# A fourth inner product cut into seven in five of seven outer products, and the small sums on one engine

## The chip, the core and the metric

The kernel runs on one core of a Trainium2 chip. The metric is the device time of one execution in microseconds. A core has five engines that each work through their own program in order: TensorE (PE, matrix multiplications into PSUM), VectorE (DVE), ScalarE (ACT), GpSimd (POOL) and SyncE (SP, which here issues the DMAs). They wait for each other by semaphores.

## The reference, cut to what matters

Input x is 64 sequences of 64 tokens of 1024 numbers, 4096 tokens in all, float32 throughout. Two layers follow each other:

```
x = x + A[id] (B[id] x)                      # rank 16, one adapter per sequence
logits = Wr x + 5 * onehot(language)         # 8 experts
gates = softmax of the top two, else 0
x = x + W x + 2 * sum_e gate_e * Bm_e (A1_e x)   # W is 1024 x 1024
```

Nearly all of the arithmetic is W x (the kernel multiplies by W + I, which takes in the residual).

## The kernel before, in words

Tokens lie along the free dimension, features on the partitions. The 4096 tokens are eight blocks of 512, and two blocks at a time make a pass (`s` = 0 to 3, `NSUP` = 4). In a pass the product (W + I) x is done by a scheme of seven multiplications in the place of eight, nested three deep:

- Outer level: W is a 2 x 2 of quarters, and the operand is a 2 x 2 of two feature halves by two token blocks. Seven *outer products* `n`, in the order `ORDER = (1, 2, 6, 7, 5, 3, 4)`, multiply sums of quarters by sums of token blocks (`token_sum`). Their results go to SBUF accumulators `U` and `V` (tiles u, v) and to output tiles `o`.
- Inner level: each outer product is again done in seven *inner products* `k` (function `product`), each of 256 x 256 weights by 256 tokens: four multiplications of 128 x 128 weights by 256 columns. The inner sums of tokens are tiles `ti` (`inner_tokens`, on POOL after pass 0). The results gather in PSUM tiles `pa` and `pb`, and DVE adds them to the accumulators (function `leave`; ACT copies where there is nothing to add to).
- Third level, in passes 1 to 3 (`FINE` = 1): the inner product `k` = 2 is cut into seven again, the *finer product* (`fine_product`, PSUM tile `pf`): seven multiplications of 128 x 128 weights by 128 columns, in four parts (four, one, one, one) between which other products stand. After each of the first three parts ACT copies a finished block to SBUF (tile `cp`), because that block has to be added in a second place; at the end DVE adds `pf` to the accumulator (`leave`), and then three sums add the blocks of `cp` (`rest_`). Ahead of it three sums make the token differences `tt` (`begin_fine`), and the weight sums `sf` are needed (`fine_weights`): they are made on POOL in pass 1, kept in DRAM (`f_kept`), and loaded in passes 2 and 3.

In outer products 2, 3, 7 and 4 the gated low-rank term is added by more multiplications of 256 columns (`b_sb` with tiles hg, hd, he) into the same PSUM tile for `k` = 2, 3, 7 and 4.

Beside this, each pass prepares the next token blocks on TensorE: transposes of the gathered B rows (`pt`), a projection (`pb` with 32-wide strips), the adapter product (`px`, from the gathered A rows `ga`, four PSUM banks at once), the expert rows (`ph`) and the transposed gates (`pg`).

The inner weight sums (tiles `s`) are made in pass 0, kept in DRAM (`s_kept`) and streamed back in every later pass, through a ring of SBUF places. `slots` gives each tile name its number of buffers: among others 26 for the weights `s` (which `sf` shares), 2 each for `tt`, `cp`, `ga`; in PSUM 4 banks `l`, 2 `a` and 2 `b`.

The order of work is not written by hand. Each step is put in by `plan.add` with an estimated cost per engine, its reads and writes, its buffers and a due time `at`; `Plan.order` runs through them with those estimates and gives every engine one fixed order, and `Pinned` keeps it. Whatever the estimates say, an engine on the chip waits for the step that stands next.

Of the kernel before, what the change touches and what calls it, by code (L numbers as in the profile page):

```python
# [8 lines left out]
F32 = mybir.dt.float32  # L9
# [5 lines left out]
P = 128  # L15
# [166 lines left out]
def kernel(  # L182
# [71 lines left out]
    WHOLE = {(0, 1)}  # L254

    FINE = 1

    pe, dve = Pinned(tc, nc.tensor), Pinned(tc, nc.vector)
    act, pool, sp = Pinned(tc, nc.scalar), Pinned(tc, nc.gpsimd), Pinned(tc, nc.sync)
    engine = {"DVE": dve, "POOL": pool}  # L260

    slots = {
        "q": 7, "s": 26, "tt": 2, "cp": 2, "t5": 2, "t6": 2, "t7": 2, "t4": 2, "o": 3, "hg": 3, "hd": 3,
        "gb": 2, "ga": 2, "bt": 1, "bx": 1, "h": 1, "l": 4, "a": 2, "b": 2,
    }
    plan = Plan(slots, {"l"})
    const = ctx.enter_context(tc.tile_pool(name="const", bufs=1))
# [6 lines left out]
    def new(tag, shape, name):  # L274
        return pools[tag].tile(shape, F32, tag=tag, name=name)
# [387 lines left out]
    }  # L663
    m_q = {1: quarter[0, 0], 2: quarter[0, 1], 4: quarter[1, 1]}
    s_kept = tc.dram_tile([7, 7, P, QC * QO], F32, name="s_kept")
    f_kept = tc.dram_tile([7, P, QC * QO], F32, name="f_kept")

    def combine(out, a, b, op, at, engines):

# [33 lines left out]
    def weights(s, n, at):  # L703

        out = {}
        if s > 0:
            for i, m in enumerate(ORDER):
                out[m] = t = ("s", s, n, m)

                def fn(e, t=t, m=m):  # L710
                    made[t] = new("s", [P, QC, QO], f"s_{s}_{n}{m}")
                    sp.dma_start(made[t].rearrange("p c o -> p (c o)"), s_kept[n - 1, m - 1])

                plan.add({"SP": 0.1}, fn, [("kept", n, m)], [(t,)], at + i - 8, [("s", t)], kb=256)
            wt[n] = out
            if s >= FINE:
                fine_weights(s, n, out[2], at)
            return
        m = m_q[n]
        out = {1: m[0, 0], 2: m[0, 1], 4: m[1, 1]}  # L720
        for k, (u, v, op) in {
            5: ((1, 0), (1, 1), ALU.add),
            6: (5, (0, 0), ALU.subtract),
            7: ((0, 0), (1, 0), ALU.subtract),
            3: ((0, 1), 6, ALU.subtract),
        }.items():
            out[k] = ("s", s, n, k)
            uu = m[u] if isinstance(u, tuple) else out[u]
            vv = m[v] if isinstance(v, tuple) else out[v]
            combine(out[k], uu, vv, op, at - 4, POOL)  # L730
        for k in ORDER:
            t = out[k]

            def keep(e, t=t, k=k):
                sp.dma_start(s_kept[n - 1, k - 1], made[t].rearrange("p c o -> p (c o)"))

            plan.add({"SP": 0.1}, keep, [(t,)], [("kept", n, k)], at + 4, kb=256)
        wt[n] = out

    def fine_weights(s, n, a, at):  # L740

        t = ("sf", s, n)

        def blocks():
            made[t] = new("s", [P, QC, QO], f"sf_{s}_{n}")
            return made[t].rearrange("p c (o w) -> p (c o) w", w=P)

        def load(e):
            blocks()
            sp.dma_start(made[t].rearrange("p c o -> p (c o)"), f_kept[n - 1])  # L750

        def sums(e):
            f, w4 = blocks(), made[a].rearrange("p c (o w) -> p (c o) w", w=P)
            a11, a21, a12, a22 = (w4[:, x] for x in range(4))
            v = engine[e]
            v.tensor_tensor(f[:, 0], a21, a22, ALU.add)
            v.tensor_tensor(f[:, 1], f[:, 0], a11, ALU.subtract)
            v.tensor_tensor(f[:, 2], a11, a21, ALU.subtract)
            v.tensor_tensor(f[:, 3], a12, f[:, 1], ALU.subtract)

        def keep(e):
            sp.dma_start(f_kept[n - 1], made[t].rearrange("p c o -> p (c o)"))

        if s == FINE:
            plan.add({"POOL": 1.6}, sums, [(a,)], [(t,)], at - 3, [("s", t)], sb=True)
            plan.add({"SP": 0.1}, keep, [(t,)], [("fine", n)], at + 4, kb=256)
        else:
            plan.add({"SP": 0.1}, load, [("fine", n)], [(t,)], at - 6, [("s", t)], kb=256)
        wt[n]["fine"] = t


    def token_sum(s, n, at):
# [80 lines left out]
    def products(s):  # L853
# [10 lines left out]
        def at():  # L864
            return s * SLOTS + slot[0]
# [104 lines left out]

        fine = {}

        def begin_fine(n):

            t, (tx, tk) = ("tt", s, n), ti[n][2]

            def fn(e):
                made[t] = new("tt", [P, 4, P], f"tt_{s}_{n}")
                f, b = made[t], tx()
                b11, b21 = b[:, 0, :P], b[:, 1, :P]  # L980
                dve.tensor_tensor(
                    f[:, :2], b[:, :, P:], b[:, 0, :].rearrange("p (h t) -> p h t", t=P), ALU.subtract
                )
                dve.tensor_tensor(f[:, 2], f[:, 1], b11, ALU.add)
                dve.tensor_tensor(f[:, 3], b21, f[:, 2], ALU.subtract)

            plan.add({"DVE": 0.9}, fn, tk, [(t,)], at() - 3, [("tt", t)], sb=True)

        def fine_product(n, part_):


            ps, cp = ("pc", s, n), ("cp", s, n)
            a, f, t, (tx, tk) = wt[n][2], wt[n]["fine"], ("tt", s, n), ti[n][2]
            extra = hd[n][2] if n in (2, 3, 7, 4) and part_ == 3 else None
            oh = {2: 0, 3: 0, 7: 1, 4: 1}.get(n)

            def fn(e):
                if part_ == 0:
                    made[ps] = new("b", [P, QC, HT], f"pf_{s}_{n}")
                out = made[ps].rearrange("p o (h t) -> p (o h) t", t=P)  # L1000
                w4 = made[a].rearrange("p c (o w) -> p (c o) w", w=P)
                a11, a21, a12, a22 = (w4[:, x] for x in range(4))
# [14 lines left out]
                    )  # L1017
                if extra is not None:
                    for j in range(QC):
                        o = oh * 2 * QC + j  # L1020
                        pe.matmul(
                            made[ps][:, j], b1_sb[:, o * P : (o + 1) * P], extra[0](),
                            start=False, stop=True, skip_group_check=True,
                        )
# [1 line left out]
            reads = [(a,), (f,), (t,)] + tk + ([("b1",), extra[1]] if extra is not None else [])  # L1026
            plan.add(
                {"PE": (0.88, 0.22, 0.22, 0.22)[part_] + 0.86 * (extra is not None)}, fn, reads,
                [(ps,)], at(), [("b", ps)] * (part_ == 0),
            )  # L1030
            slot[0] += (0.5, 0.13, 0.13, 0.13)[part_]

            def copy(e):
                out = made[ps].rearrange("p o (h t) -> p (o h) t", t=P)
                if part_ == 0:

                    made[cp] = new("cp", [P, 4, P], f"cp_{s}_{n}")
                    act.copy(made[cp][:, 0::3], out[:, 1::2])
                else:
                    act.copy(made[cp][:, part_], out[:, 1])  # L1040

            if part_ < 3:
# [2 lines left out]
                    [(cp,)], at() - 4, [("cp", cp)] * (part_ == 0),  # L1045
                )
                return
            leave(n, ps, 0, ALL, (0,), True)
            region = qk(dest[n], 0, ALL, (0,))

            def rest_(e):
                o, c = q(dest[n], 0, ALL, (0,)), made[cp]
                c11, c21, c2 = o[:, 0, :P], o[:, 1, :P], o[:, 1]
                dve.tensor_tensor(c11, c11, c[:, 0], ALU.add)
                dve.tensor_tensor(c2, c2, c[:, 1:3].rearrange("p h t -> p (h t)"), ALU.add)
                dve.tensor_tensor(c21, c21, c[:, 3], ALU.add)

            plan.add({"DVE": 0.9}, rest_, [(cp,)] + region, region, at() - 4, sb=True)

        def done(n, i, cs, js):  # L1060

# [39 lines left out]
        def begin(n):  # L1101
# [10 lines left out]
                    gate_diff(s, at() - 2)  # L1112
                return
            inner_tokens(s, n, tokens[n], at())
            if s >= FINE:
                begin_fine(n)
            if n == 4:
                gate_diff(s, at() - 2)
            if n in (2, 7, 3, 4):
# [2 lines left out]
        def step(n, k):  # L1122
# [8 lines left out]
            if k in (1, 6, 5, 3):  # L1131
# [4 lines left out]
                    leave(n, ("pb2", s, n), 1, ALL, (1,), True)  # L1136
                if k == 5 and last(n):
                    leave(n, ps, 0, ALL, (1,))
            elif k == 2:
                product(n, ("pc", s, n), 2, True)  # L1140
                leave(n, ("pc", s, n), 0, ALL, (0,), True)
            else:
                product(n, ("pb2", s, n), k, k == 7)
                if k == 7 and last(n):
                    leave(n, ("pb2", s, n), 1, ALL, (1,))
                if k == 4:
                    leave(n, ("pb2", s, n), 1, ALL, (0,), True)
# [1 line left out]
                done(n, i, ALL, (j,))  # L1149


        whole_h = {}
        begin(ORDER[0])
        rest = []
        for n in ORDER:
            after = ORDER[ORDER.index(n) + 1] if n != ORDER[-1] else None
            if (s, n) in WHOLE:
# [5 lines left out]
                    if x == 1 and after is not None:  # L1163
                        begin(after)
                continue
            step(n, 1)
            if rest:
                step(*rest[0])
            if s >= FINE:
                fine_product(n, 0)  # L1170
            else:
                step(n, 2)
            if rest:
                step(*rest[1])
            if after is not None:
                begin(after)

            for x, k in enumerate((6, 7, 5)):
                if s >= FINE:
                    fine_product(n, 1 + x)  # L1180
                if s >= FINE and x == 2:
                    done(n, 0, ALL, (0,))
                step(n, k)
            rest = [(n, 4), (n, 3)] if last(n) else [(n, 3), (n, 4)]
        for k in rest:
            step(*k)

    for k, at in ((0, -60), (1, -42)):
        load(k, 0, at)
# [86 lines left out]
```

## Time and profile before

| | |
|---|---|
| median of 3 runs | 519.69 us (519.22 to 520.44) |
| the profiled execution | 518.82 us, of which the profile's span is 517.0 |
| TensorE busy | 502.6 us (97% of the span) |
| VectorE busy | 359.2 us (69%) |
| GpSimd busy | 183.8 us (36%) |
| ScalarE busy | 59.1 us (11%) |
| granted TensorE clock | full in all of the span |
| DMA | 104.73 MB, mean 203 GB/s |

All of the kernel's instructions are recorded under one line (L29), that of the helper `Pinned`, so the profile is read by tile names: `pa<-ti,s` is a multiplication into `pa` of token sums `ti` and weights `s`. A TensorE multiplication in float32 leaves two records, so an inner product of four is "x8". Start and duration are in us, those of single instructions in ns. The passes can be told apart by time: pass 0 until about 147 us, then 123 us each.

### The profile page before, as it was taken

Reading aid. Unit: us, or ns where it says so; the run is one execution under the profiler, and the core shown is the slowest. Engines: PE = TensorE matmul, PEld = TensorE weight load, DVE = VectorE, ACT = ScalarE, POOL = GpSimd, SP = SyncE. Lnnn points to the kernel's source line nnn. Section 1 sums busy time; section 2 is a strip of 40 time slices with the busy share of each in tenths; the row PEclk is TensorE's granted clock in tenths of the full one; section 3 lists DMA queues with packets and bytes.
Section 4 is the critical chain, followed back from the end, with each engine's and each line's share of the span. In section 5 each row is a group of like instructions: output and inputs, shape, how many; then the busy total and the mean of one; then the engine's idle time right before and its main releaser. Section 6 shows DMA issues by size and latency. Waiting matters only on the chain.

```text
span 517.0 us, 9064 instructions
## 1 busy us (share of the span) xinstructions
PE 502.6 (97%) x3558; PEld 441.3 (85%) x3558; DVE 359.2 (69%) x700; ACT 59.1 (11%) x144; POOL 183.8 (36%) x169
## 2 busy tenths in 40 slices
PE   2999999999999999999999999999999999999997
PEld 2857988889889988898888898899889899888886
DVE  0689998988853596656888558548679558654843
ACT  1111100002001111012101110101200111001100
POOL 4073058182534346333234303312423332524300
PEclk9999999999999999999999999999999999999999
DMA  7999275798576347926466724954655674660122
GB/s 260 372 367 402 89 264 215 269 327 289 178 236 221 102 124 273 364 96 213 175 204 223 226 103 128 370 175 116 210 184 153 180 219 114 212 183 22 57 107 81
DMA packets 57290, 104.73 MB, mean 203 GB/s; under 512 B 5280, under 2 KB 11424, under 8 KB 57248
## 3 DMA queue, kind: packets, MB, share of 16 engines
q1 hardware_dynamic: 54944, 95.77, 54.8%
q0 software_dynamic: 2304, 8.39, 4.7%
q8 instruction: 28, 0.46, 0.3%
q14 instruction: 14, 0.11, 0.1%
HBM read 72.68 MB, written 31.46 MB: 201 GB/s over the span
## 4 chain that ended last, share of the span: by engine, by line
PE 92%; DVE 3%; DMA 2%; issue 1%; POOL 1%; SPq 0%; POOLq 0%
PE pa L29 37%; PE pb L29 28%; PE ph L29 11%; PE pf L29 8%; PE px L29 3%; PE pw L29 3%; DMA x<-in_xT 2%; DVE o L29 1%; PE pt L29 1%; DVE t L29 1%; PE pg L29 1%; POOL ti L29 0%; DVE x L29 0%; DVE tt L29 0%; SPq L29 0%
## 5 line engine op out<-in xcount | busy, mean ns | idle before, releaser
L29 PE MATMUL pa<-ti,s 128*128 128x256 f32 x432 | 102.6, 381 | 0.0
L29 PE MATMUL pb<-ti,s 128*128 128x256 f32 x384 | 95.7, 380 | 0.1
L29 PEld LDWEIGHTS pa<-ti,s 128*128 128x128 f32 x432 | 79.4, 190 | 10.0 <-issue 0.2
L29 PEld LDWEIGHTS pb<-ti,s 128*128 128x128 f32 x384 | 70.5, 190 | 8.7 <-DVE o L29 0.3
L29 PE MATMUL ph<-a_sb,x 128*128 128x136 f32 x512 | 63.0, 279 | 0.2 <-issue 0.2
L29 PEld LDWEIGHTS ph<-a_sb,x 128*128 128x128 f32 x512 | 62.0, 190 | 1.1 <-issue 0.4
L29 POOL TENSOR_TENSOR ti<-x,ti 128x512 f32<-128x512 f32 x24 | 32.2, 1340 | 71.6 <-PE pb L29 70.7
L29 POOL TENSOR_TENSOR ti<-x 128x512 f32<-128x512 f32 x24 | 31.6, 1316 | 67.9 <-PE pb L29 44.0
L29 PE MATMUL pa<-x,s 128*128 128x256 f32 x216 | 52.0, 380 | 0.0
L29 DVE TENSOR_TENSOR x<-px,x 128x512 f32<-128x512 f32 x64 | 39.6, 682 | 11.7 <-PE px L29 8.3
L29 POOL TENSOR_TENSOR ti<-t,ti 128x512 f32<-128x512 f32 x18 | 25.6, 1421 | 55.9 <-PE pb L29 55.1
L29 PEld LDWEIGHTS pa<-x,s 128*128 128x128 f32 x216 | 39.8, 190 | 5.0 <-issue 0.2
L29 PE MATMUL pa<-t,s 128*128 128x256 f32 x168 | 41.1, 381 | 0.0
L29 ACT COPY cp<-pf 128x128 f32<-128x128 f32 (+1 forms) x63 | 19.0, 302 | 182.4 <-PE pf L29 161.8
L29 POOL TENSOR_TENSOR ti<-t 128x512 f32<-128x512 f32 x18 | 23.4, 1299 | 36.5 <-PE pb L29 29.3
L29 PEld LDWEIGHTS pa<-t,s 128*128 128x128 f32 x168 | 31.3, 190 | 4.3 <-issue 0.2
L29 DVE TENSOR_TENSOR o<-pb,o 128x512 f32<-128x512 f32 x35 | 24.1, 689 | 13.6 <-PE pb L29 12.8
L29 POOL TENSOR_TENSOR s<-w,w 128x512 f32<-128x512 f32 x12 | 17.1, 1428 | 35.5 <-DVE w L29 22.3
L29 DVE TENSOR_TENSOR o<-pa,u 128x512 f32<-128x512 f32 x32 | 21.9, 686 | 5.8 <-PE pa L29 4.3
L29 PE MATMUL pf<-tt,sf 128*128 128x128 f32 x126 | 24.6, 277 | 0.0
L29 PEld LDWEIGHTS pf<-tt,sf 128*128 128x128 f32 x126 | 21.7, 191 | 2.1
L29 DVE TENSOR_TENSOR x<-x,x 128x512 f32<-128x512 f32 x16 | 12.5, 798 | 12.6 <-PE ph L29 12.6
(141 smaller groups left out, 728.0 us busy)
## 6 DMA issues: line engine op xcount, KB each, us to landing
s<-s_kept SPq DMA_DIRECT2D x147, 256.0 KB, 3.3
x<-in_xT SPq DMA_DIRECT2D x15, 1024.0 KB, 7.7
out_T<-o SPq DMA_DIRECT2D x30, 512.0 KB, 3.1
s_kept<-s SPq DMA_DIRECT2D x28, 256.0 KB, 4.3
s_kept<-w SPq DMA_DIRECT2D x18, 256.0 KB, 5.4
w<-in_w SPq DMA_DIRECT2D x16, 256.0 KB, 8.0
sf<-f_kept SPq DMA_DIRECT2D x14, 256.0 KB, 2.7
f_kept<-sf SPq DMA_DIRECT2D x7, 256.0 KB, 3.6
```

Of the source, the lines that this page charges most:

```text
L29: return self._tc.keep_in_program_order(f(*args, **kwargs))
```

## The change: what it does

In outer products 1, 2, 6, 7 and 3 the inner product `k` = 4 is done as a finer product too, in passes 1 to 3 (list `FOURTH`; its PSUM tile comes from the banks `l`, its token side is the sum `ti` of `k` = 4). The last outer product of the last pass is excepted by a test, but 4 is not in the list.

The sums `tt` and the late additions of `cp` run on POOL for all finer products, where they ran on DVE. Weight sums `sf` are kept for two `k` per outer product. `s` gets a 27th place, `tt` and `cp` a third one, `ga` loses its second.

The interleaving changes as well: a list `going` holds the finer products that are under way, and `advance()` issues the next part of each after every inner product, so that the fourth's parts run on into the next outer product.

```diff
+    FOURTH = (1, 2, 6, 7, 3)
...
-        "q": 7, "s": 26, "tt": 2, "cp": 2, "t5": 2, "t6": 2, "t7": 2, "t4": 2, "o": 3, "hg": 3, "hd": 3,
-        "gb": 2, "ga": 2, "bt": 1, "bx": 1, "h": 1, "l": 4, "a": 2, "b": 2,
+        "q": 7, "s": 27, "tt": 3, "cp": 3, "t5": 2, "t6": 2, "t7": 2, "t4": 2, "o": 3, "hg": 3, "hd": 3,
+        "gb": 2, "ga": 1, "bt": 1, "bx": 1, "h": 1, "l": 4, "a": 2, "b": 2,
...
-    f_kept = tc.dram_tile([7, P, QC * QO], F32, name="f_kept")
+    f_kept = tc.dram_tile([7, 2, P, QC * QO], F32, name="f_kept")
+
+    def fine_of(s, n):
+
+        return ((2, 4) if n in FOURTH and (s, n) != (NSUP - 1, ORDER[-1]) else (2,)) if s >= FINE else ()
...
-            if s >= FINE:
-                fine_weights(s, n, out[2], at)
+            for k in fine_of(s, n):
+                fine_weights(s, n, k, out[k], at + (k == 4) * 5)
...
-                dve.tensor_tensor(f[:, 2], f[:, 1], b11, ALU.add)
-                dve.tensor_tensor(f[:, 3], b21, f[:, 2], ALU.subtract)
-
-            plan.add({"DVE": 0.9}, fn, tk, [(t,)], at() - 3, [("tt", t)], sb=True)
+                v.tensor_tensor(f[:, 2], f[:, 1], b11, ALU.add)
+                v.tensor_tensor(f[:, 3], b21, f[:, 2], ALU.subtract)
+
+            plan.add({"POOL": 1.7}, fn, tk, [(t,)], at() - 3, [("tt", t)], sb=True)
...
+            ps, cp, tag = ("pf", s, n, k), ("cp", s, n, k), "b" if k == 2 else "l"
...
-            plan.add({"DVE": 0.9}, rest_, [(cp,)] + region, region, at() - 4, sb=True)
+            plan.add({"POOL": 1.7}, rest_, [(cp,)] + region, region, at() - 4, sb=True)
+            done(n, row, ALL, (0,))
...
+        def advance():
+            for u in list(going):
+                fine_product(*u)
+                u[2] += 1
+                if u[2] == 4:
+                    going.remove(u)
...
+                step(n, 1)
+                going.append([n, 2, 0])
+                advance()
+                for k in rest:
+                    step(*k)
+                    advance()
+                if after is not None:
+                    begin(after)
+
+                for k in (6, 7, 5):
+                    step(n, k)
+                    if k == 7 and 4 in fine_of(s, n):
+                        going.append([n, 4, 0])
+                    advance()
+                if 4 in fine_of(s, n):
+                    rest = [(n, 3)]
+                    continue
```

More of the change, by code (lines that the diff above doesn't have):

```diff
@@ L738, in weights, with fine_weights @@
         wt[n] = out
-    def fine_weights(s, n, a, at):
-        t = ("sf", s, n)
+    def fine_weights(s, n, k, a, at):
+        t, kept = ("sf", s, n, k), f_kept[n - 1, k // 4]
         def blocks():
-            made[t] = new("s", [P, QC, QO], f"sf_{s}_{n}")
+            made[t] = new("s", [P, QC, QO], f"sf_{s}_{n}{k}")
             return made[t].rearrange("p c (o w) -> p (c o) w", w=P)
@@ L749, in load @@
             blocks()
-            sp.dma_start(made[t].rearrange("p c o -> p (c o)"), f_kept[n - 1])
+            sp.dma_start(made[t].rearrange("p c o -> p (c o)"), kept)
         def sums(e):
@@ L761, in keep @@
         def keep(e):
-            sp.dma_start(f_kept[n - 1], made[t].rearrange("p c o -> p (c o)"))
+            sp.dma_start(kept, made[t].rearrange("p c o -> p (c o)"))
         if s == FINE:
             plan.add({"POOL": 1.6}, sums, [(a,)], [(t,)], at - 3, [("s", t)], sb=True)
-            plan.add({"SP": 0.1}, keep, [(t,)], [("fine", n)], at + 4, kb=256)
+            plan.add({"SP": 0.1}, keep, [(t,)], [("fine", n, k)], at + 4, kb=256)
         else:
-            plan.add({"SP": 0.1}, load, [("fine", n)], [(t,)], at - 6, [("s", t)], kb=256)
-        wt[n]["fine"] = t
+            plan.add({"SP": 0.1}, load, [("fine", n, k)], [(t,)], at - 6, [("s", t)], kb=256)
+        wt[n]["fine", k] = t
     def token_sum(s, n, at):
@@ L971, in products, with begin_fine, fine_product @@
         fine = {}
-        def begin_fine(n):
-            t, (tx, tk) = ("tt", s, n), ti[n][2]
+        def begin_fine(n, k):
+            t, (tx, tk) = ("tt", s, n, k), ti[n][k]
             def fn(e):
-                made[t] = new("tt", [P, 4, P], f"tt_{s}_{n}")
-                f, b = made[t], tx()
+                made[t] = new("tt", [P, 4, P], f"tt_{s}_{n}{k}")
+                f, b, v = made[t], tx(), engine[e]
                 b11, b21 = b[:, 0, :P], b[:, 1, :P]
-                dve.tensor_tensor(
+                v.tensor_tensor(
                     f[:, :2], b[:, :, P:], b[:, 0, :].rearrange("p (h t) -> p h t", t=P), ALU.subtract
                 )
-                dve.tensor_tensor(f[:, 2], f[:, 1], b11, ALU.add)
-                dve.tensor_tensor(f[:, 3], b21, f[:, 2], ALU.subtract)
-            plan.add({"DVE": 0.9}, fn, tk, [(t,)], at() - 3, [("tt", t)], sb=True)
[L989 to L995, printed above, removed]
+                v.tensor_tensor(f[:, 2], f[:, 1], b11, ALU.add)
+                v.tensor_tensor(f[:, 3], b21, f[:, 2], ALU.subtract)
+            plan.add({"POOL": 1.7}, fn, tk, [(t,)], at() - 3, [("tt", t)], sb=True)
+        def fine_product(n, k, part_):
+            ps, cp, tag = ("pf", s, n, k), ("cp", s, n, k), "b" if k == 2 else "l"
+            a, f, t, (tx, tk) = wt[n][k], wt[n]["fine", k], ("tt", s, n, k), ti[n][k]
+            extra = hd[n][k] if n in (2, 3, 7, 4) and part_ == 3 else None
+            oh, row = {2: 0, 3: 0, 7: 1, 4: 1}.get(n), k // 4
             def fn(e):
                 if part_ == 0:
-                    made[ps] = new("b", [P, QC, HT], f"pf_{s}_{n}")
+                    made[ps] = new(tag, [P, QC, HT], f"pf_{s}_{n}{k}")
                 out = made[ps].rearrange("p o (h t) -> p (o h) t", t=P)
@@ L1019, in fn @@
                     for j in range(QC):
-                        o = oh * 2 * QC + j
+                        o = (oh * 2 + row) * QC + j
                         pe.matmul(
@@ L1028, in fine_product @@
                 {"PE": (0.88, 0.22, 0.22, 0.22)[part_] + 0.86 * (extra is not None)}, fn, reads,
-                [(ps,)], at(), [("b", ps)] * (part_ == 0),
+                [(ps,)], at(), [(tag, ps)] * (part_ == 0),
             )
@@ L1035, in copy @@
                 if part_ == 0:
-                    made[cp] = new("cp", [P, 4, P], f"cp_{s}_{n}")
+                    made[cp] = new("cp", [P, 4, P], f"cp_{s}_{n}{k}")
                     act.copy(made[cp][:, 0::3], out[:, 1::2])
@@ L1047, in fine_product @@
                 return
-            leave(n, ps, 0, ALL, (0,), True)
-            region = qk(dest[n], 0, ALL, (0,))
+            leave(n, ps, row, ALL, (0,), True)
+            region = qk(dest[n], row, ALL, (0,))
             def rest_(e):
-                o, c = q(dest[n], 0, ALL, (0,)), made[cp]
+                o, c, v = q(dest[n], row, ALL, (0,)), made[cp], engine[e]
                 c11, c21, c2 = o[:, 0, :P], o[:, 1, :P], o[:, 1]
-                dve.tensor_tensor(c11, c11, c[:, 0], ALU.add)
-                dve.tensor_tensor(c2, c2, c[:, 1:3].rearrange("p h t -> p (h t)"), ALU.add)
-                dve.tensor_tensor(c21, c21, c[:, 3], ALU.add)
-            plan.add({"DVE": 0.9}, rest_, [(cp,)] + region, region, at() - 4, sb=True)
+                v.tensor_tensor(c11, c11, c[:, 0], ALU.add)
+                v.tensor_tensor(c2, c2, c[:, 1:3].rearrange("p h t -> p (h t)"), ALU.add)
+                v.tensor_tensor(c21, c21, c[:, 3], ALU.add)
+            plan.add({"POOL": 1.7}, rest_, [(cp,)] + region, region, at() - 4, sb=True)
+            done(n, row, ALL, (0,))
         def done(n, i, cs, js):
@@ L1114, in begin @@
             inner_tokens(s, n, tokens[n], at())
-            if s >= FINE:
-                begin_fine(n)
+            for k in fine_of(s, n):
+                begin_fine(n, k)
             if n == 4:
@@ L1138, in step @@
                     leave(n, ps, 0, ALL, (1,))
+                if k == 5 and 4 in fine_of(s, n):
+                    leave(n, ("pb2", s, n), 1, ALL, (0,), True)
             elif k == 2:
@@ L1149, in step @@
                 done(n, i, ALL, (j,))
-        whole_h = {}
+        whole_h, going = {}, []
+        def advance():
[4 more added lines that the diff above has]
+                    going.remove(u)
         begin(ORDER[0])
@@ L1165, in products @@
                 continue
[L1166 to L1170, printed above, removed]
-            else:
[L1172 to L1183, printed above, removed]
+            if s < FINE:
+                step(n, 1)
+                if rest:
+                    step(*rest[0])
+                step(n, 2)
+                if rest:
+                    step(*rest[1])
+                if after is not None:
+                    begin(after)
+                for k in (6, 7, 5):
+                    step(n, k)
+            else:
+                step(n, 1)
+                going.append([n, 2, 0])
[3 more added lines that the diff above has]
+                    advance()
+                if after is not None:
+                    begin(after)
+                for k in (6, 7, 5):
+                    step(n, k)
+                    if k == 7 and 4 in fine_of(s, n):
[4 more added lines that the diff above has]
+                    continue
             rest = [(n, 4), (n, 3)] if last(n) else [(n, 3), (n, 4)]
@@ L1186, in products @@
             step(*k)
+            advance()
+        while going:
+            advance()
     for k, at in ((0, -60), (1, -42)):
```

## The prediction

> **What bounds the kernel now.** I read the page first (busy shares and the chain that ended last), then busy time by stretch, then TensorE's timeline, then single tiles, then the waits. The page:
>
> ```profile
> span 517.0 us, 9064 instructions
> ...
> PE 502.6 (97%) x3558; PEld 441.3 (85%) x3558; DVE 359.2 (69%) x700; ACT 59.1 (11%) x144; POOL 183.8 (36%) x169
> ...
> PE 92%; DVE 3%; DMA 2%; issue 1%; POOL 1%; SPq 0%; POOLq 0%
> ```
>
> TensorE is 92% of the chain; a busy PE alone would prove little, since its ends are modelled. By stretch (start, passes 0 to 3; columns busy us and count, granted clock, DMA share, GB/s):
>
> ```profile
> 20.00:147.00 127.00, 126.98 (x972) 105.53 (x972) 115.82 (x220) 11.32 (x24) 56.47 (x47) 1.00 0.77 271
> 147.00:270.00 123.00, 123.00 (x906) 110.03 (x905) 78.63 (x158) 15.37 (x39) 50.70 (x52) 1.00 0.60 201
> 270.00:393.00 123.00, 122.87 (x901) 110.05 (x900) 84.95 (x169) 15.90 (x41) 37.33 (x28) 1.00 0.57 189
> 393.00:517.00 124.00, 120.50 (x632) 107.84 (x630) 74.98 (x143) 12.90 (x35) 33.64 (x25) 1.00 0.41 132
> ```
>
> The reader should see that in passes 1 to 3, the only ones that change, PE has no idle microsecond at clock 1.00, while DVE (65%), ACT (13%) and POOL (30 to 41%) have room. What those passes cost is what TensorE issues. Its price list, from the chain in order of time and from TensorE's timeline:
>
> ```profile
> 183.00 0.22 PE pf L29 x2
> ...
> 189.07 1.73 PE pa L29 x8
> 190.80 0.89 PE pf L29 x8
> ...
> 198.60 0.22 PE pf L29 x2
> ```
>
> An inner product is four multiplications (two records each, x8) of 256 columns: 1.73 us, 0.4325 each. Four fine multiplications of 128 columns (part 0) take 0.89 and a single one 0.22.
>
> **Part 1: TensorE (removes work on the path).** The order of instructions confirms that 15 more products (five outer products in three passes) come as seven multiplications of 128 columns. Each costs 0.89 + 3 x 0.22 = 1.55 instead of 1.73: 0.18 saved. The gate multiplications (256 columns, outer 2, 7, 3) stay. 15 x 0.18 = **2.7 us**. If 128 columns cost exactly half of 256, 7 x 0.216 = 1.51 and 3.2; if every piece paid 0.225, 2.3.
>
> Here a rule speaks against the change. The Trainium skill, "TensorE: Matmul & The Clock Gate", section "Back-to-back issue gap", gives 81 ns per multiplication at N=128 and 131 at N=512 in a sustained stream: halving the columns does not halve the cost. On a straight line between these, N=256 is 98 ns, so seven of 128 against four of 256 cost 567 to 391, 45% more. Scaled to 1.73 us that would be +0.78 a product, +11.7 us in all (an estimate from that page). This trace's rows say 0.22 to 0.4325, a ratio of 0.51, and they are the same instructions in the same kernel, so I take the rows.
>
> **Part 2: sums that go from DVE to POOL (off the path, if Pool keeps up).** Per finer product there are two groups of three sums (the token differences tt, the late additions of cp), each 256+128+128 columns. Now there are 21 such products on DVE; then 36, all on Pool. One row of DVE, three of Pool:
>
> ```profile
> L29 DVE TENSOR_TENSOR tt<-x,tt x12: 291/396/1318, 120.5 to 467.1; 128x128 f32<-128x128 f32 x12
> ...
> L29 POOL TENSOR_TENSOR ti<-x x24: 1262/1268/1556, 135.0 to 465.5; 128x512 f32<-128x512 f32 x24
> ...
> L29 POOL TENSOR_TENSOR sf<-s x14: 448/459/897, 115.0 to 229.8; 128x128 f32<-128x128 f32 x14
> ...
> L29 POOL TENSOR_TENSOR sf<-sf,s x7: 455/456/787, 115.6 to 229.4; 128x128 f32<-128x128 f32 x7
> ```
>
> Pool at 256 columns is not in the trace. It lies between 0.456 (128) and 1.268 (512); by the line between them it is 0.73, which I take. A group is 0.73 + 2 x 0.456 = 1.64; 72 groups are 118 us. The weight sums sf (four of 128 columns, 1.82) come 5 times more, in pass 1: 9 us. DVE loses 21 x 2 groups, 63.5 us by its rows (tt 34.7, cp 28.8): 21 a pass. Pool's work by pass:
> - pass 1: 50.7 + 24 x 1.64 + 9.1 = 99 us of 120 (83%)
> - passes 2 and 3: 37 + 24 x 1.64 = 76 of 120 (64%)
>
> The skill's "GPSIMD Engine Reference", section "Elementwise — side-by-side cycle accounting", says to use DVE for elementwise work, 1.96x faster at N=2048. By it a group would be 1.96 x (0.414 + 2 x 0.291) = 1.95 and pass 1 107 us (89%); the trace's ratio is 1.85 at 512 columns and 1.57 at 128, hence my 1.64. Neither reaches 120, so the rule costs nothing while Pool's lateness is absorbed.
>
> Does it arrive in time? I added the TensorE costs along the new order and looked for the places where Pool has least room. The worst is outer product 7 of pass 1. On TensorE's own scale (0 at its first multiplication), a token buffer comes free at 181.3. Pool then has three ti sums (3.8), a cp group, a tt group, a cp group (4.9), three ti (3.8), sf (1.8), one ti (1.3), a cp group (1.6): 17.3 us, done at 198.6. DVE needs the last group for its sum of pa and U, released at 198.6, and the PSUM bank of pa is wanted at 203.6. DVE's sum takes 0.69, so 4.3 us are spare: Pool may be 1.25 times slower than undisturbed before TensorE stands. In this trace Pool's 84 ti sums average 1.34 against a median of 1.27, 1.06 times. So I price this at 0. If that cover goes, the loss is the excess over 4.3 us, once a pass.
>
> **Part 3: waits that the new order puts closer.** ACT gets 45 more copies (15 x (0.37 + 2 x 0.27) = 14 us on an engine busy 11%). Two kinds of PSUM handoff are shorter now. Part 0 and part 1 of a fourth product stand 0.87 us apart in some places, with a 0.37 or 0.27 copy between; the present order already has such gaps without a hole in PE: 0. In outer product 2 of each pass, DVE must empty pa between two of its products with 1.09 us of other TensorE work between (one full product, 1.73, in the nearest place now): the sum takes 0.69 and leaves 0.4 for two semaphore hops and for DVE being elsewhere. Bounds 0 and 0.7 each; I take 0.1 each: **+0.3 us**.
>
> **Part 4: queues and buffers.**
> - SP: 5 more stores in pass 1 and 10 more loads after it, 256 KB each (0.32 us of SP each, 2.7 us to landing), at a DMA share of 0.6. The weight ring has 27 places for 61 loads a pass (26 for 56): it still runs some 53 us ahead. 0; bound +0.5.
> - The A-row buffer ga is single. Block 1's gather, issued at 11.3 now, must wait for block 0's last px (ends 17.3), lands at most 8.5 later (longest of the 8), at 25.9, and is first used at 31.9. Behind it on Pool are weight sums that began only at 28.6, waiting for DVE. Block 3's gather moves from 45 to about 111; its use is at 129.7. 0; bound +0.5.
> - The fourth product takes a bank of "l", shared with px, which needs all four: already in the order that I summed; 0 to 0.5 a pass.
>
> Sum: -2.7 + 0.3 = -2.4. The profiled execution (span 517.0, own time 518.82) would come to 516.4; the median shown, 519.69, is 0.9 above it, so I predict **517.3**.
>
> **Rivals.**
> 1. *Handoffs eat most of it.* Closer order, same PE work. At 0.7 us for each of the three pa places and 0.5 for px in each pass: 3 x 1.2 = 3.6 worse than no waits, which alone would use up the gain; half of that gives 518.8. For: PE has no slack, so every late release shows. Against: DVE falls from 65% to about 48% of these passes, so it is more often free when a bank ends.
> 2. *Pool becomes the bound in pass 1 (slower).* Place: the run of sums in outer 7, then every later one, since the sums stand in one queue. Price: 99 us undisturbed; Pool then has to be 1.21 times slower to fill 120, and 1.25 times to lose 3.7 us, which turns the gain into a loss that can be measured. At 1.28: 127 us, +7, 523.5. For: DVE and Pool do disturb each other when both read SBUF twice (DVE's 128-column sum up to 1318 ns against 291; Pool's weight sums in pass 0, where DVE is 91% busy, average 1.43, 1.13 times). Against: after the change DVE has fewer such sums, so Pool should be disturbed less than in pass 0.
> 3. *128 columns cost as the page says*: 531. Only a hidden limit on weight loads could do it; the four-in-a-row at 0.89 excludes it.
> That the change doesn't do what it says is excluded by the order of instructions.
>
> **How the numbers follow.** Forecast 0.70 (516.3 to 518.5); rival 1 0.16 (518.5 to 519.9); rival 2 0.13 (521 to 526); rival 3 0.01. A measurement here can tell about 0.2%, 1.04 us, from no change: faster means under 518.65. Faster 0.70 + 0.05 of rival 1 = 0.75; same 0.11; slower 0.14. The range 516.2 to 519.9 leaves out rivals 2 and 3 and a little at the low end (a gain of 3.2 with no wait).
>
> **What would show it.** Right: in the new trace passes 1 to 3 are each about 0.8 us shorter with PE still full; pf in groups of 0.89 and 0.22; POOL about 310 us busy, 83% in pass 1; DVE about 300. Wrong: idle PE before pf or pa released by POOL tt, ti or DVE u/o (rivals 2 and 1); Pool's 128-column mean well over 0.55; DVE waiting for POOL u, o, v for more than a few microseconds in total; or px waiting for DMA ga.

## The result and the profile after

| | before | after |
|---|---|---|
| median of 6 runs each | 519.46 us (519.15 to 520.48) | 516.58 us (516.04 to 517.08) |
| ratio | | 0.9939, 95% interval 0.9928 to 0.9951 |
| the profiled execution (its span) | 518.82 (517.0) | 517.08 (515.3) |

The change makes the kernel 0.6% faster. The profiled execution of after is at the slow end of its runs: its first projection took 1.97 us where that of before took 1.11 (the first `PE pb` step of the chain, at 13.8 us in both). This varies from one execution to the next: the same kernel profiled again (experiment e5) took 1.44 there and had a span of 514.6.

The page of after, first the busy shares, then the chain that ended last by engine:

```profile
span 515.3 us, 9478 instructions
...
PE 501.1 (97%) x3648; PEld 441.6 (86%) x3648; DVE 329.3 (64%) x589; ACT 71.4 (14%) x189; POOL 318.7 (62%) x405
...
PE 97%; DMA 2%; DVE 0%; issue 0%; SPq 0%; POOL 0%
```

POOL went from 36% to 62% of the span, and still no step of the chain that matters is POOL's; DVE's 3% of the chain are gone. Busy time by stretch, roughly passes 1 to 3 (columns: stretch, its length; busy us and count of PE, PEld, DVE, ACT, POOL; granted clock, DMA share, GB/s):

```profile
147.00:270.00 123.00, 123.00 (x932) 110.56 (x931) 75.28 (x133) 19.58 (x55) 95.50 (x130) 1.00 0.62 215
270.00:393.00 123.00, 122.99 (x932) 110.38 (x931) 74.52 (x135) 19.77 (x56) 80.17 (x101) 1.00 0.61 204
393.00:515.00 122.00, 118.72 (x668) 107.41 (x666) 61.70 (x100) 17.18 (x51) 76.05 (x100) 1.00 0.45 145
```

TensorE is as full as before, at clock 1.00. The PE counts rise by 26 to 36 a stretch, where the stretch is as long or shorter: more multiplications of half the columns. POOL is at 95.5 us in pass 1, 78% of the stretch. Its new instructions, by tile (min/median/max ns):

```profile
L29 POOL TENSOR_TENSOR tt<-ti x15: 719/726/1053, 149.9 to 474.3; 128x256 f32<-128x256 f32 x15
...
L29 POOL TENSOR_TENSOR tt<-ti,tt x15: 453/456/785, 151.5 to 475.7; 128x128 f32<-128x128 f32 x15
```

The estimate for 256 columns was 0.73, and 0.726 came; 128 columns stayed at 0.456.

**Two quantities used below.** To see small differences I priced TensorE's work in each trace: each multiplication at its price from the chain (0.4325 us for 256 columns, 0.2225 for 128 in a finer product, and likewise for the other kinds), added along the order. The *price sum* is what TensorE has to issue. The *remainder* is the time from 25 us to the last multiplication less the price sum from there: holes (times in which TensorE stands), changes between kinds of multiplication, and clock. Starting at 25 us leaves out the start-up just told of. Here a pass begins on TensorE with its first inner product, at 153.8, 280.4 and 404.6 us in before and at 154.6, 283.4 and 407.2 in after. The stretches that begin at 147, 270 and 393 only come near the passes.

| us | price sum | remainder | of it in pass 0 / 1 / 2 / 3 |
|---|---|---|---|
| before | 494.95 | 5.25 | 2.22 / 1.78 / 1.10 / 0.15 |
| after | 492.36 | 5.19 | 2.21 / 1.42 / 1.64 / -0.08 |

From the multiplication that stands at 25 us in before to the last one, after takes 2.65 us less: by these prices 2.59 of it is the multiplications, and 0.06 all else.

### The profile page after: what moved, and what is told of

It reads as the page before. It is cut to its first block, busy times and chain, and to the rows that moved or that the text cites. A ratio compares the mean times of both kernels' runs of the same rounds, so it can differ in the third digit from the quotient of the medians.

```text
span 515.3 us, 9478 instructions
## 1 busy us (share of the span) xinstructions
PE 501.1 (97%) x3648; PEld 441.6 (86%) x3648; DVE 329.3 (64%) x589; ACT 71.4 (14%) x189; POOL 318.7 (62%) x405
## 4 chain that ended last, share of the span: by engine, by line
PE 97%; DMA 2%; DVE 0%; issue 0%; SPq 0%; POOL 0%
PE pa L29 39%; PE pb L29 23%; PE pf L29 15%; PE ph L29 12%; PE px L29 3%; PE pw L29 3%; DMA x<-in_xT 2%; PE pt L29 1%; PE pg L29 1%; DVE o L29 0%; SPq L29 0%; DVE bx L29 0%; POOL x L29 0%
## 5 line engine op out<-in xcount | busy, mean ns | idle before, releaser
L29 PE MATMUL pb<-ti,s 128*128 128x256 f32 x264 | 65.6, 380 | 0.0
L29 ACT COPY cp<-pf 128x128 f32<-128x128 f32 (+1 forms) x108 | 32.2, 302 | 201.0 <-PE pf L29 189.1
L29 PEld LDWEIGHTS pb<-ti,s 128*128 128x128 f32 x264 | 48.6, 190 | 5.9
L29 POOL TENSOR_TENSOR o<-o,cp 128x128 f32<-128x128 f32 (+1 forms) x54 | 34.5, 651 | 20.9 <-DVE o L29 15.6
L29 PE MATMUL pf<-tt,sf 128*128 128x128 f32 x216 | 42.1, 278 | 0.0
L29 PEld LDWEIGHTS pf<-tt,sf 128*128 128x128 f32 x216 | 35.5, 191 | 3.2 <-issue 0.8
```

Of the source, the lines that this page charges most:

```text
L29: return self._tc.keep_in_program_order(f(*args, **kwargs))
```

## The experiments

Ratios are to the kernel before on the same chip, with a 95% interval; they are estimated from all the runs, and can differ by about 0.1% from the quotient of the two medians. Medians of before were 519.21 (e1 to e4), 519.41 (e5 to e8) and 519.00 (e9 to e11). Theory A is that the gain is the cheaper fourth products alone, the sums being free on POOL; the rivals are that the move of the sums, or the new order and buffers, bring it.

### e1, e7: without the fourth products; e3, e6: with the sums back on DVE

```diff
-    FOURTH = (1, 2, 6, 7, 3)
+    FOURTH = ()            # e1, e7, and e6
```
```diff
-            plan.add({"POOL": 1.7}, fn, tk, ...      # tt
+            plan.add({"DVE": 0.9}, fn, tk, ...
...
-            plan.add({"POOL": 1.7}, rest_, ...       # additions of cp
+            plan.add({"DVE": 0.9}, rest_, ...        # both: e3, e6
```

> The changed kernel with an empty list of fourth products: small sums on Pool, buffers and interleaving as changed, but TensorE issues as many multiplications as before. Theory (the gain is 15 products times 0.18 us of TensorE, all else costs nothing): 519.2 us, within 0.5 of the kernel before, passes of TensorE work full. Rival (freeing DVE of 63 us of sums gives part of the gain): 518 or less. Rival (the moves cost something that the multiplications hide): 520.5 or more.

> The changed kernel with the tt sums and the late additions of cp on DVE again, for all 36 finer products. Theory (either engine has the room): DVE gets 24 groups of about 1.5 us a pass, 75 + 36 = 111 of 122 us in passes 1 and 2, Pool falls to some 60 and 45; TensorE stays full or nearly, 516.5 to 518.5. Rival (the move to Pool is what makes the fourth product pay): DVE's sums from PSUM come late, banks are not free, 519.5 or more.

> The changed kernel with no fourth products and all small sums on DVE: of the change only buffers and interleaving are left. Theory (the kernel before loses about 1 us in small holes because DVE is late, and the move to Pool takes that away): within 0.6 of the kernel before, 518.9 to 519.8. Rival (the new interleaving or the buffers bring the 1.6 us, not Pool): 517.7, as with no fourth products and sums on Pool.

> No fourth products, sums on Pool, once more beside the others. Theory: 517.6, 1.0 to 1.6 over the changed kernel. Rival (its first result was chance): 519 or more.

e5 is the changed kernel once more, as the fourth corner beside e6 and e7:

> The changed kernel itself once more, beside the three others on one chip. Theory now (fifteen fourth products save 2.6 us of TensorE's own work; Pool takes the sums without delaying TensorE): 516.5, ratio to before 0.994. Against the kernel with no fourth products, which came out 1.6 us under the kernel before, it should be 1.0 to 1.6 lower. Rival (the fourth products are worth next to nothing and the Pool sums bring it all): equal to the kernel with no fourth products within 0.4 us.

Measured, with price sum and remainder of each trace:

| fourth products | sums on | median us | ratio | price sum | remainder |
|---|---|---|---|---|---|
| none (e6) | DVE | 518.40 | 0.9972 [0.9961, 0.9983] | 494.95 | 4.21 |
| none (e7) | POOL | 518.11 | 0.9967 [0.9956, 0.9978] | 494.95 | 4.17 |
| none (e1) | POOL | 517.66 | 0.9958 [0.9942, 0.9974] | 494.95 | 4.16 |
| five (e3) | DVE | 518.03 | 0.9979 [0.9965, 0.9992] | 492.36 | 8.23 |
| five (e5, the change) | POOL | 516.29 | 0.9937 [0.9924, 0.9950] | 492.36 | 5.20 |

Three things follow.

First, e6 has neither of the two announced parts, and is still 0.28% under before (1.4 us by the ratio, 1.0 by the medians). The expectations of e1 (519.2) and e6 (518.9 to 519.8) missed this; the rival named for e6, interleaving or buffers, came. What is left in it are the buffers (a third `tt` and `cp`, a 27th weight, one `ga`), the interleaving with `going`, and the order that follows from them. Its remainder is 1.04 us smaller. Part of that is one hole of before, in outer product 4, the last of pass 1. Before's chain in order of time there (start, us, what):

```profile
271.40 2.88 DVE t L29 x3
274.27 0.61 DVE o L29
...
274.93 2.86 PE pb L29 x12
```

DVE's sum of `o` stands behind three token sums `t`, and TensorE stands for 0.29 us until it comes. In e1, e6 and e7 there is no hole over 0.12 us in these passes. Another part is one change fewer between strips and whole multiplications (23 returns for 24, about 0.34 us; the price is told at e10). The other 0.4 stays open, and buffers and interleaving were not tried apart.

Second, moving the sums alone (e6 to e7, same chip) is worth 0.3 us, inside both intervals: 0, as it was priced. Pass 1 of e7 shows why it is neither gain nor loss: PE is full, DVE was not the bound and POOL is at 58%.

```profile
147.00:270.00 123.00, 123.00 (x894) 110.01 (x893) 66.86 (x130) 15.63 (x40) 71.25 (x91) 1.00 0.62 204
```

Third, the fourth products are worth 1.8 us with the sums on POOL (e7 to e5, same chip, by medians; by the ratios 1.6; by the traces 2.59 - 1.03 = 1.56; by e1 and the first measurement of after, as ratios, 1.0) and nothing with them on DVE (e6 0.9972, e3 0.9979). So the two parts belong together: with five fourth products and the sums on DVE, DVE is late. (e3 lies in the range of its theory, 516.5 to 518.5; that it gains nothing shows only beside e6.) Pass 1 of e3, and the chain at one of its holes in pass 3:

```profile
147.00:270.00 123.00, 121.41 (x922) 109.08 (x921) 95.16 (x196) 19.35 (x53) 56.29 (x64) 1.00 0.64 212
```
```profile
467.10 1.25 DVE tt L29
...
468.38 1.31 DVE tt L29
469.69 0.61 DVE v L29
...
470.35 2.86 PE pa L29 x12
```

and POOL's timeline there:

```profile
466.75 1.44 POOL L29 TENSOR_TENSOR ti<-x 128x512 f32<-128x512 f32 x1 [1.97 <-PE pa L29]
468.27 1.27 POOL L29 TENSOR_TENSOR ti<-x,ti 128x512 f32<-128x512 f32 x1
```

DVE is at 77% of the stretch, and its 128-column sums, 0.29 us at the median, take 1.25 and 1.31 here, with the `v` that TensorE needs behind them: 0.78 us lost at this place, 0.52 at another. Each of the two long sums ends 0.15 us after a sum of POOL's (468.35 after 468.19, 469.69 after 469.54). Moving the sums also gives another order of work (TensorE's order in e3 is not that of after), so e3 tests engine and order together; another order with the sums on DVE was not tried. (The profiled execution of e3, 519.70, is above its median: 1.24 us of idle TensorE at 218.5 are a wait for a load of x.)

### e2, e8: seven and six fourth products

```diff
-    FOURTH = (1, 2, 6, 7, 3)
+    FOURTH = (1, 2, 6, 7, 5, 3, 4)     # e2; e8: (1, 2, 6, 7, 5, 3)
```

> The changed kernel with the fourth product cut in all seven outer products (5 more products; the very last is excepted). Theory (TensorE alone counts while Pool has room): 5 x 0.18 = 0.9 us less than the changed kernel, about 515.7; Pool in pass 1 rises from 95 to some 106 us of 122 (two tt and two cp groups at 1.64, two sf at 1.82). Rival (Pool's queue is already the limit at 85%): pass 1 gets longer by several microseconds, 518 or more.

> Fourth products in outer products 1, 2, 6, 7, 5 and 3, sums on Pool. With all seven, TensorE's own work was 0.9 less but holes of 0.5 to 1.1 us appeared, most of them around outer product 4. Theory (outer 4 at the seam of two passes, where DVE makes the token sums, is what doesn't bear it): 0.5 us less than the changed kernel, 516.0. Rival (any more Pool work costs more than the 3 x 0.18 us saved): 516.8 or more.

Measured: e2 518.00, ratio 0.9983 [0.9961, 1.0005]; e8 517.84, ratio 0.9965 [0.9953, 0.9978]. Both theories (515.7 and 516.0) missed. Both are slower than five, though TensorE has less to issue: price sums 491.50 and 491.84 against 492.36, remainders 8.61 and 6.84 against 5.19. Where it went in e8 can be read from its chain near the end of pass 3:

```profile
491.83 0.27 ACT cp L29
...
492.15 2.26 PE pf L29 x14
...
494.51 0.38 ACT cp L29
...
494.93 0.49 PE pf L29 x2
```

Two finer products are under way and nothing else is left to stand between their parts, so the next part waits for ACT's copy of the part before: 0.52 and 0.70 us with the ends of the pipeline, 1.2 us lost in pass 3 alone for 0.52 us of price. e2 has the same two holes, and 1.14 us at 277.2 where DVE's `t` sums were late, and 0.6 at 152.5 where an output tile was not yet stored.

### e4: double POOL's token differences

```diff
+                for _ in range(2):
                     v.tensor_tensor(f[:, :2], ...
                     v.tensor_tensor(f[:, 2], f[:, 1], b11, ALU.add)
                     v.tensor_tensor(f[:, 3], b21, f[:, 2], ALU.subtract)
```

> The changed kernel with each group of three tt sums computed twice on Pool (the same values), in the same order on every engine: 12 x 1.64 = 20 us more Pool work in each of passes 1 to 3, so 115 of 123 us in pass 1 and 97 in passes 2 and 3. Theory (Pool has 4.3 us to spare at its tightest run, in outer product 7 of pass 1, and binds from 1.21 to 1.25 times its work): a loss of 0 to 3 us, pass 1 alone, 516.5 to 519.5. Rival (Pool's slack is much larger since PE would only stand when Pool is full for a whole pass): no loss. Rival (Pool is late in every pass already): 20 us or more lost in all, 535.

Measured: 527.44, ratio 1.0161 [1.0137, 1.0185]: 11 us above the change, where at most 3 and pass 1 alone were expected. Passes 1 and 3:

```profile
147.00:270.00 123.00, 120.31 (x915) 107.42 (x914) 74.62 (x128) 19.34 (x53) 113.63 (x165) 1.00 0.59 208
...
393.00:524.00 131.00, 123.35 (x689) 110.63 (x687) 67.70 (x105) 18.19 (x54) 96.66 (x134) 1.00 0.44 139
```

In pass 1 POOL is 92% busy, and the remainder grows by 4.4 us. But in pass 3 it grows by 5.7, with POOL busy in 74% of the stretch. The largest hole, 2.52 us, lies there. Its chain:

```profile
489.29 1.11 POOL o L29 x2
...
490.95 1.75 DVE u L29
...
494.28 0.69 DVE o L29
...
495.02 1.99 PE pa L29 x8
```

and on DVE's timeline the sum between `u` and that `o`:

```profile
492.73 1.63 DVE L29 TENSOR_TENSOR o<-v,o 128x512 f32<-128x512 f32 x1
```

POOL comes late out of a run of its own sums, DVE's `u` waits for it and then takes 1.75 (its median in after is 1.04), the next sum takes 1.63 (0.85 at the median of after), and TensorE waits for the `o` behind them. POOL's share of a pass does not tell where this happens. A run of sums in one place does.

### e9: one local run, made longer

The prediction named the tightest place, outer product 7 of pass 1, with 4.3 us to spare. e9 repeats the token differences of that one finer product.

```diff
+                for _ in range(6 if (s, n, k) == (1, 7, 4) else 1):
                     v.tensor_tensor(f[:, :2], ...
```

> The changed kernel with one group of tt sums (outer 7, product 4, pass 1) computed six times on Pool instead of once, same values, same order: 5 x 1.64 = 8.2 us more in the one run of Pool work that the prediction called the tightest, and nothing elsewhere; Pool in pass 1 at 104 of 123 us (84%). Theory (what counts is the slack of the run, 4.3 us, not Pool's share): TensorE stands for about 8.2 - 4.3 = 4 us at the second pa of outer 7 (near 220 us), total 519 to 521. Rival (a queue with 15% idle absorbs it before the pass ends): no hole, 516.5. Rival (as in the kernel with all tt twice, the loss sits at the end of pass 3 only): no loss in pass 1.

Measured: 522.91, ratio 1.0077 [1.0053, 1.0101]. TensorE's timeline (start, us, what; in brackets the idle time before and its releaser), then DVE's:

```profile
210.81 0.39 PE L29 MATMUL pf<-tt,sf 128*128 128x128 f32 x2
215.71 3.78 PE L29 MATMUL pa<-ti,s 128*128 128x256 f32 x8 [4.51 <-DVE v L29]
219.43 1.92 PE L29 MATMUL px<-bx,ga 32*128 32x128 f32 x32
```
```profile
214.97 0.69 DVE L29 TENSOR_TENSOR v<-pa,u 128x512 f32<-128x512 f32 x1 [8.96 <-POOL u L29]
```

The hole is at the place that the prediction named: `pa` of outer product 7 waits for DVE, which waits for POOL's additions to U. POOL was given 9.0 us more (327.7 busy for 318.7); TensorE lost 4.7 in the hole, so some 4.3 were absorbed, about what the prediction had counted as spare. The total, 522.91, lies above the 519 to 521 that were expected: the pass lost more than the hole. Its remainder is 8.73 for 1.42, 7.3 us more. The stretches of the hole and after it say why:

```profile
211.00:215.70 4.70, 0.20 (x2) 0.01 (x1) 0.73 (x2) 0.27 (x1) 4.39 (x9) 0.84 0.99 352
215.70:220.00 4.30, 4.29 (x16) 3.10 (x20) 1.35 (x3) 0.00 (x0) 4.14 (x6) 0.50 0.72 266
214.20:221.00 6.80, 5.29 (x36) 4.10 (x40) 2.08 (x4) 0.00 (x0) 6.56 (x10) 0.50 0.70 258
```

In the hole of 4.5 us the granted clock went to 0.50, and it stayed there until about 221.0, 5.3 us after TensorE had work again: by starts the product at 215.71 took 3.72 (215.71 to 219.43) in the place of 1.73. Half a clock for 5.3 us loses 2.65, which with the 4.7 of the hole makes up the 7.3. In e4, with holes up to 2.5 us, the clock of each pass stayed 1.00. The Trainium skill, "TensorE: Matmul & The Clock Gate", section "What's actually happening", has the array fall to half clock after an idle window of about 3.4 us and come back after a busy one of the same length; e4 and e9 lie on either side of it. In e9 the clock fell 3.0 us into the hole (at 214.2) and came back after 5.3 us of work, so the 3.4 is only a rough guide here.

### e10, e11: both halves of a projection together; a sixth fourth product where it has company

In after's traces TensorE loses a little time where it goes over to the 32-wide strips of a projection and back. In after's timeline the two halves of a projection stand apart:

```profile
206.90 1.08 PE L29 MATMUL pb<-x,bt 128*32 128x128 f32 x32
207.91 0.49 PE L29 MATMUL pf<-tt,sf 128*128 128x128 f32 x2
208.23 0.61 PE L29 MATMUL pf<-t,s 128*128 128x128 f32 x4
...
209.12 1.89 PE L29 MATMUL pa<-t,s 128*128 128x256 f32 x8
210.95 1.08 PE L29 MATMUL pb<-x,bt 128*32 128x128 f32 x32
```

e10 issues both halves in one step for blocks 2 and on. e11 adds a fourth product in outer product 5 to it, except in the last pass.

```diff
-        for h in range(2):
+        if k > 1:
             plan.add(
-                {"PE": 0.94}, lambda e, h=h: fn(range(h * HC, (h + 1) * HC)),
+                {"PE": 1.88}, lambda e: (fn(range(HC)), fn(range(HC, NC))),
...
-        return ((2, 4) if n in FOURTH and ...
+        return ((2, 4) if (n in FOURTH or (n == 5 and s < NSUP - 1)) and ...     # e11 only
```

> The changed kernel with the two halves of each projection (32-wide strips) standing together on TensorE from block 2 on, so that TensorE goes back from strips to whole multiplications 22 times instead of 25. Theory (each return costs 0.2 us): TensorE's time over its price list falls by 0.6 us in the trace, 515.7 to 516.2. Rival (the order shifts and other holes open): no gain, 516.4 or more.

> As the one before, and the fourth product of outer 5 cut as well in passes 1 and 2 only (in pass 3 it opened two holes of 0.5 and 0.7 us where no other product was left to stand between the parts): 2 x 0.18 us more saved. Theory: 515.3 to 515.9. Rival (more Pool work opens holes at the seam of passes 1 and 2): 516.5 or more.

Measured: e10 515.10, ratio 0.9919 [0.9902, 0.9937]; e11 515.14, ratio 0.9922 [0.9905, 0.9939], both a little below the ranges of their theories. Beside the change (0.9939 and 0.9937) e10 is some 0.9 us faster by ratio; the intervals overlap, but the traces agree with it: same price sum, remainder 4.18 for 5.19. The same place in e10:

```profile
208.05 1.96 PE L29 MATMUL pb<-x,bt 128*32 128x128 f32 x64
209.93 0.49 PE L29 MATMUL pf<-ti,sf 128*128 128x128 f32 x2
210.26 0.39 PE L29 MATMUL pf<-tt,sf 128*128 128x128 f32 x2
```

By starts, a half costs 1.01 us (206.90 to 207.91), and two together 1.88, 0.14 less than two halves; and the first pair of 128 columns after strips takes 0.32 or 0.33 (207.91 to 208.23), where one that follows others takes 0.22. The whole product before strips takes 1.83 by starts (209.12 to 210.95), where elsewhere it takes 1.73. These three differences, 0.14, 0.10 and 0.10, are the price of one more trip to strips and back: 0.34 us. e10 has three returns from strips fewer (22 for 25), and 1.01 us less remainder, 0.34 for each. Both ways of reckoning agree.

e11 has 0.34 us less to issue than e10 and 0.11 more remainder; the 0.2 that is left is under what the runs can tell, and they show none of it. The sixth fourth product does no harm where other work stands between its parts (e11), and harm where none does (e8). e10 is the fastest kernel here.

## Why the prediction was right

**The sum.** 517.3 was predicted against a median of 519.69, a ratio of 0.9954; measured were 516.58 and 0.9939. It was right to 0.8 us. The term that carries it, TensorE's cheaper products, is shown by the runs. That the whole came so near is in part luck: two terms of about 1 us each, with opposite signs, were not in the sum (Part 4).

**Part 1, TensorE: right.** 2.7 us were predicted. The price sum fell by 2.59; it is worked out from prices too, but the measured time over the same multiplications fell by about as much (2.65). It was said to come as 0.8 in each pass. That cannot be read from the passes' lengths: they went from 126.7, 124.2 and 108.5 us to 128.8, 123.8 and 104.1, since the new order also moves other work from one pass to another. Chain rows of after, the products that stayed whole and the pieces of 128 columns:

```profile
164.52 1.73 PE pb L29 x8
166.25 1.11 PE pf L29 x10
```

A whole product is still 1.73, and five multiplications of 128 columns take 1.11, 0.22 each. The figures of the Trainium skill, "TensorE: Matmul & The Clock Gate", section "Back-to-back issue gap", from which the prediction estimated 11.7 us more, do not fit the float32 multiplications here: 0.22 to 0.4325 us was measured, and rival 3 is excluded.

**Part 2, the sums: the price 0 was right, and the place of danger too.** POOL was predicted to be about 310 us busy, 99 of them in pass 1; it is 318.7 and 95.5. The 4.3 us spare in outer product 7 are about what e9 found, and after has 4.0 there: DVE's sum that waits for POOL's U is done at 208.44, and TensorE wants the bank at 212.51.

```profile
207.75 0.69 DVE L29 TENSOR_TENSOR v<-pa,u 128x512 f32<-128x512 f32 x1 [0.35 <-POOL u L29]
```
```profile
212.51 1.89 PE L29 MATMUL pa<-ti,s 128*128 128x256 f32 x8
```

In all of after DVE waits for POOL's U before `v` twice, the longer time in pass 3 (2.0 us, at 459.7), and TensorE does not stand behind it:

```profile
DVE v L29 <- POOL u L29: 2.3, 2, 2.0
```

Where Part 2 fell short is in what it left unsaid: the sums cost nothing on POOL but cannot stay on DVE (e3). The move is not a neutral part beside the gain; without it, in the order of e3, the gain of the fourth products is 0.

DVE was predicted at 300 and is 329. Of these 29 us, 10 are 15 more additions of `pf` (0.69 each), which the working missed: a fourth product with its own PSUM tile is added to its accumulator by itself. Much of the rest is sums with two SBUF inputs that take longer than before (those of 512 columns 128 us for 117); they lie off the path.

**Part 3, handoffs: 0 for +0.3.** There is no hole at the `pa` handoffs of outer product 2 in any trace of the change. The only one over 0.12 us in after's passes is 0.17 at 363.2, at `pg`. Rival 1 needs such holes and is excluded.

**Part 4: 0 was right for queues and `ga`; the sign of its bounds was wrong.** It bounded buffers and order by a loss only. e6 shows them to be a gain of 1.0 us in the remainder (1.0 by the medians, 1.4 by the ratio). In the change this does not show, because the fourth products give back the same 1.03 (remainder 4.17 in e7, 5.20 in e5): two more returns from strips, 25 for 23, at 0.34 each, the hole of 0.17 at 363.2, which e7 does not have, and about 0.2 whose cause stays open. A term of -1.0 and one of +1.0 were missing, and their sum hid both: this is the luck in the number.

**Rival 2, POOL as the bound: not here, but near.** e4 and e9 are this rival made to happen. Its mechanism, as they show it, is a run of POOL sums in front of DVE's sum in front of TensorE's bank. Its measure, the share of pass 1, was the wrong one: e4 lost most in pass 3 at 74%.

## What to carry to other kernels

When an engine issues all the time, count what it issues by its own durations: that count held here, while what lay between instructions moved by as much as 1 us in either direction and has to be priced both ways. Work moved to an idle engine is to be tested by its tightest local run against the next consumer, not by that engine's share of a stage. And a part that gains nothing alone can be what lets another part gain: only the four corners of a two-part change show it.

## What the runs showed of the hardware that was not expected

**Sums with two SBUF inputs stretch; sums with one from PSUM do not.** After's DVE tiles (min/median/max):

```profile
L29 DVE TENSOR_TENSOR o<-pa,u x32: 676/692/693, 53.6 to 499.0; 128x512 f32<-128x512 f32 x32
...
L29 DVE TENSOR_TENSOR u<-u,o x16: 679/1039/1755, 102.8 to 487.9; 128x512 f32<-128x512 f32 x16
```

Before:

```profile
L29 DVE TENSOR_TENSOR u<-u,o x16: 676/684/1657, 101.9 to 488.3; 128x512 f32<-128x512 f32 x16
```

In every run the sum with one input from PSUM stays at 0.69; the other has long cases in every run too. The Trainium skill, "SBUF — State Buffer", section "SBUF: two separate sides", has DVE and POOL share a pair of ports that one instruction holds for its whole length, for a DVE operation with two SBUF inputs. These rows agree, and so does e3, where DVE's long sums end 0.15 us after sums of POOL's. POOL's total work does not set the median, though: with POOL busy for 342 us in e2 and 382 in e4 it was 846 and 906, below the 1039 of after with 319. That it depends on which sums meet, and so on the order, is likely but not shown. POOL pays as well: its 84 `ti` sums take 1.34 on average before and 1.33 after, against a median of 1.27.

**A long hole is paid for again after its end.** 4.7 us of idle TensorE in e9 cost 7.3, because the clock was halved until 5.3 us after it.

**Going over to strips and back costs about 0.34 us** (e10), which no busy share shows, since the engine counts as busy.
